# Two attention layers on one core: float32r softmax sums, a two-part order for the last batch, a separate block for the first normalisation, and weight sums by VectorE

## The chip, the core and the metric

The kernel runs on one core of one Trainium2 chip. A time is the device time of one execution, in microseconds (us). Engines are named as in the profile: PE is TensorE's matmul queue and PEld its weight loads, DVE is VectorE, ACT is ScalarE, POOL is GpSimd, SP is SyncE, which here only issues transfers.

## What is computed

The input is x of shape 8 x 32 x 32 x 512, float32: 8 batches of N = 1024 tokens with C = 512 channels. Two layers follow each other; each adds to x an attention over a normalised x. The normalisation has 32 groups of 16 channels and no learned scale.

```python
x = x + L0(group_norm(x))     # qkv = xn @ w_qkv; 16 heads of 32; softmax(q k^T / sqrt(32)) v; @ w_proj + b_proj
x = x + L1(group_norm(x))     # q, k, v = xn @ Wq, Wk, Wv; 4 heads of 128;
                              # softmax(q k^T / sqrt(128) + relative position logits) v; @ Wo
```

## The kernel before, in words

**Products.** All eight 512 x 512 products of a batch (q, k, v and the projection of each layer) are done as 2 x 2 block products with seven multiplications instead of eight. The activations need four combined blocks, made by four VectorE operations in `forms` (L327, operations L339 to L342); the weights need four sums each, made once by `Matrix.add_up` (L137, operation L146) and stored to DRAM, from where `Stream` (L167) fetches the tiles that each product needs, seven products ahead, on SyncE's queue (L193, L197). The first layer's three matrices are kept on chip for the first batch (`keep`). `seven` (L348) runs the seven products of one half in the order of `ORDER`, 0, 5, 1, 4, 6, 2, 3, into three PSUM banks x, y and z; VectorE, ScalarE and GpSimd drain them (`Plain` L405 and `Onto` L430). Products 0 and 1 read only the blocks a11 and a12, which are the activations themselves; 5, 4, 6, 2 and 3 read at least one combined block or a block of the second half of the tokens.

**Attention.** `attention_0` (L526) works on four heads at once: 8 score matmuls (L539) into a four-bank PSUM tile `ps`, one exponential on ScalarE (L547), 4 matmuls with v (L558), and a VectorE addition that keeps the sum of the exponentials (L567, L569). `attention_1` (L644) works on one head and 512 queries: for each of 8 blocks of 128 keys, a score matmul (L654, float32), a matmul that adds the position logits (L655, float32r: the constant `sel` and `posT`), an exponential (L657), a matmul with v (L666) and an addition (L675, L677). When the 8 blocks are done, `finish` multiplies the exponentials' sums by a matrix of ones (L686, float32), which adds them over partitions, and `normalise` (L496) turns them into reciprocals and multiplies (L502 to L524).

**Order.** Round b of the loop at L958 runs the first layer's attention of batch b beside everything else (`side_by_side`, L883): the projection of batch b-1 (`after_0`), the output projection of batch b-2 (`after_1`), the second layer's q, k, v of batch b-1 (`second`), its attention, and the loading and q, k, v of batch b+1. `side_by_side` takes steps from the rest according to costs that each part yields (2 for each pair of matmul groups); the second attention yields 0, so outside the round b = 7 it runs without first-layer steps in between. In round 7 its first 32 of 64 blocks run beside the first attention; in round 8 there is no first attention at all. `woven` (L871) mixes a side part into a main part at a given start and gap. Within these limits each engine's queue is put in order by when work is expected to be ready, and `issue_after` adds that an instruction comes after a given one on its engine.

**Start and end.** `load_first` (L726) brings batch 0 as rows, transposes them on PE, copies them with ScalarE and VectorE (L752, L754), takes statistics (L249), stores x (`put_away`, L214), normalises in place (L294) and makes the forms. Then the sums of WV0 are made by GpSimd, those of WQ0 and WK0 by VectorE (L939 to L942). `before_first` runs the first halves of v, q and k. The sums of the other five matrices are made by GpSimd during the q, k, v of batch 1 (`other_sums`, L946, woven at L1002). At the end `after_1` projects the last batch: forms, then twice seven products, each output block being transposed by VectorE (L856) and stored by four DMAs (L861).

Large tensors sit in eight blocks of 2 MB (`block`), so a new one waits for a free block.

Of the kernel before, what the change touches and what calls it, by code (L numbers as in the profile page):

```python
# [17 lines left out]
P = 128  # L18
# [9 lines left out]
def quick_path(  # L28
# [58 lines left out]
    ones = consts.tile([P, P], F32, tag="ones", name="ones")  # L87
    nc.gpsimd.memset(ones, 1.0)
# [28 lines left out]

    HC, HN = CC // 2, NB // 2
# [5 lines left out]
    class Matrix:  # L124
# [12 lines left out]
        def add_up(self, engine, store, keep=False):  # L137
# [5 lines left out]
            for i, (x, y) in enumerate(  # L143
                [(b12, b11), (b22, sums[:, 0]), (b22, b12), (b21, sums[:, 1])]
            ):
                engine.tensor_tensor(sums[:, i], x, y, op=ALU.subtract)  # L146
# [18 lines left out]
    ORDER = [0, 5, 1, 4, 6, 2, 3]  # L165

# [46 lines left out]

    def put_away(xT, name):  # L214
        kept = []
        for cc in range(CC):
            d = dram.tile([P, N], F32, tag="kept", name=f"d_{name}_{cc}", bufs=4 * CC)
            nc.sync.dma_start(d, xT[cc])
            kept.append(d)
        return kept  # L220
# [34 lines left out]
    def group_norm(st, xT, name, after=None, behind=None):  # L255
# [36 lines left out]
        for cc in range(CC):  # L292
            with tc.issue_after(behind().ins) if behind is not None else nullcontext():
                nc.vector.tensor_scalar(  # L294
                    xT[cc],
# [13 lines left out]
    half_done = [None]  # L309

# [16 lines left out]
    def forms(x, name, room=None):  # L327
# [11 lines left out]
        nc.vector.tensor_add(s1, a21, a22)  # L339
        nc.vector.tensor_sub(s2, s1, a11)  # L340
        nc.vector.tensor_sub(a21, a11, a21)
        nc.vector.tensor_sub(s4, a12, s2)  # L342
        return [a11, a12, s4, a22, s1, s2, a21]

# [3 lines left out]
    def seven(fs, u, rows, sink, name, hook=None):  # L348

# [17 lines left out]

        x = bank(f"x_{name}")
# [31 lines left out]
        yield HC  # L403

# [239 lines left out]
    def attention_1(q, k, v, posT, b):  # L644
# [15 lines left out]
        def back(h, c, j, e):  # L660
# [15 lines left out]
            elif j > 1:  # L676
                nc.vector.tensor_add(state["esum"], state["esum"], e)  # L677
# [5 lines left out]
        def finish(h, c, esum):  # L683
            name = f"1_{b}_{h}_{c}"
            su = bank(f"sums_{name}")
            nc.tensor.matmul(su, ones, esum, start=True, stop=True)  # L686
            normalise(q[:, h, c * NB : (c + 1) * NB], su, name)

        pending = None
        for at in steps:  # L690
            e = front(*at)
            ended = state.pop("ended", None)
# [3 lines left out]
            if ended is not None:  # L696
                finish(*ended)
# [3 lines left out]
        finish(*state.pop("ended"))  # L701

    def load(b, st):
# [3 lines left out]
        ahead = [load_blocks(b, *parts[i]) for i in range(2)]  # L707
# [15 lines left out]
        st["xn"] = forms(x, f"xn0_{b}")  # L723
        yield 0

    def load_first(st):  # L726
# [5 lines left out]
        WV0.fetch(nc.sync)  # L732
        x = block("x0T_0")
        xT = chunks(x)
        for h in range(NH):
# [13 lines left out]
            for cc in range(CC):  # L749
                part = xT[cc][:, h * NB : (h + 1) * NB]  # L750
                if h == 0 or cc % 2:
                    nc.scalar.copy(part, banks[cc])  # L752
                else:
                    nc.vector.tensor_copy(part, banks[cc])  # L754
# [4 lines left out]
        for cc in (1, 0, 3, 2):  # L759
            statistics(st, xT, cc, "0_0")  # L760
        st["kept"] = put_away(xT, "0_0")
        run(group_norm(st, xT, "0_0"))
        st["xn"] = forms(x, "xn0_0")
# [42 lines left out]
    def after_0(b, st, hook=None):  # L806

        fs = st.pop("ao0") if "ao0" in st else forms(st["q0"], f"ao0_{b}", block(f"forms_{b}"))
        x = st["x1"] = block(f"x1T_{b}")
        xT = fetch(st["kept"], x)  # L810
        for u in range(2):
            bias = [bproj_sb[:, n * HC + u : n * HC + u + 1] for n in range(2)]
            stream.unit(WP, False, u)
            yield from seven(
                fs, u, False, Onto(halves(xT, u), bias), f"wp_{b}_{u}", hook if u else None
            )
            for n in range(2):
                statistics(st, xT, n * HC + u, f"1_{b}")

# [25 lines left out]
    def after_1(b, st, hook=None):  # L845

        if "ao1" not in st:
            forms_1(b, st)
        fs = st.pop("ao1")
        xT = fetch(st["kept"], block(f"x2T_{b}"))  # L850
        for u in range(2):

            def put_out(n, h):
                m = n * HC + u
                ot = mem.tile([P, NB], F32, tag="row", name=f"ot_{b}_{m}_{h}", bufs=3)
                nc.vector.transpose(ot, xT[m][:, h * NB : (h + 1) * NB])  # L856
                ot = ot.rearrange("p (t i) -> p t i", i=32)
                for a in range(P // 32):

                    queue = nc.scalar if b == B - 1 and a % 2 else nc.sync  # L860
                    queue.dma_start(  # L861
                        by_blocks(of[b, h * NB : (h + 1) * NB, :], m * P + 32 * a),
                        ot[32 * a : 32 * a + 32],
                    )

            stream.unit(WO, False, u)
            yield from seven(
                fs, u, False, Onto(halves(xT, u), then=put_out), f"wo_{b}_{u}", hook if u else None
            )

# [50 lines left out]

    FIRST = units(WQ0) + units(WK0) + units(WV0, True)
    plan = [(m, m is WV0, u, ORDER) for u in range(2) for m in (WV0, WQ0, WK0)]
    for b in range(B + 1):
        if b >= 1:
            plan += units(WP)
# [8 lines left out]
    plan += units(WO)  # L935
# [3 lines left out]
    WV0.add_up(nc.gpsimd, nc.gpsimd, keep=True)  # L939
    for m in (WQ0, WK0):  # L940
        m.fetch(nc.sync)
        m.add_up(nc.vector, nc.gpsimd, keep=True)  # L942
# [3 lines left out]
    def other_sums():  # L946
        for m in (WP, WQ1, WK1, WV1, WO):
            m.fetch(nc.gpsimd)
            m.add_up(nc.gpsimd, nc.gpsimd)
# [7 lines left out]
    run(before_first(states[0]))  # L957
    for b in range(B + 1):  # L958
# [11 lines left out]
        if last is not None:  # L970
# [14 lines left out]
            attention = later(lambda st: attention_1(*st.pop("at")), last)  # L985
            if here is not None and coming is None:
# [8 lines left out]
            rest.append(woven(attention, incoming, 4, 6))  # L995
# [3 lines left out]
        if coming is not None:  # L999

            before = later(before_0, b + 1, coming, forms_0 if last is not None else None)
            rest.append(before if last is not None else woven(before, other_sums(), 2, 7))  # L1002
# [500 lines left out]
```

## Time and profile before

| | |
|---|---|
| runs of the kernel | 3879.32, 3877.97, 3873.93 us; median 3877.97 |
| the profiled execution, its own time | 3877.0 us |
| its span | 3875.2 us |
| mean granted PE clock | 0.996 |
| first q, k, v product (x_v, L315) starts | 27.28 us |
| first step of the first attention (ps, L539) | 67.39 us |
| last product of the last projection begins | 3863.08 us |

Busy shares are in the page's first part. A busy PE is not a PE at its peak: matmuls are pipelined and their ends are modelled, so how fast they go is read from the distance of their starts. The waits of PE list the time in which PE had nothing in flight, with what ended it. The chain of waits goes back from the last instruction to what released it.

### The profile page before, as it was taken

To read this page: it belongs to the slowest core of one execution; us is meant where nothing else is said; L and a number is where in the kernel's file an instruction comes from. 1 tells how busy PE (TensorE), PEld (TensorE's weight loads), DVE (VectorE), ACT (ScalarE), POOL (GpSimd) and SP (SyncE) were. 2 spreads that over 40 slices of the span, in tenths; PEclk is the share of its full clock that TensorE was granted. 3 is DMA by queue.
4 is the path that set the end of the run, shared out by engine and by line. 5 is a ranking of instruction groups with operands and counts; after the bars stand their busy time and mean duration, and the time that the engine had idled before them with its cause. 6 is when DMAs were issued, how large, how long until landed. Compare 5 with 4: busy or idle time off the path is not lost.

```text
span 3875.2 us, 79813 instructions
## 1 busy us (share of the span) xinstructions
PE 3803.0 (98%) x34478; PEld 1375.0 (35%) x34478; DVE 2516.4 (65%) x2905; ACT 1723.9 (44%) x1767; POOL 625.1 (16%) x400
## 2 busy tenths in 40 slices
PE   8999999999999999999999999999999999999998
PEld 3222244232443234432343323433234332334353
DVE  6777765686745867468664686656866568665544
ACT  2554543545434454344544445444453445553232
POOL 2242101121001211012111121111210112001101
PEclk9999999999999999999999999999999999999999
DMA  6122120142202322033120241103311023110401
GB/s 183 58 87 80 42 60 3 37 126 65 57 6 79 94 54 55 12 92 87 42 55 17 92 94 38 47 21 98 90 41 39 27 97 76 34 52 24 121 17 23
DMA packets 482984, 234.73 MB, mean 61 GB/s; under 512 B 269600, under 2 KB 461376, under 8 KB 481600
## 3 DMA queue, kind: packets, MB, share of 16 engines
q1 hardware_dynamic: 470992, 213.74, 20.4%
q0 software_dynamic: 2608, 13.70, 1.0%
q8 instruction: 274, 4.49, 0.5%
q10 hardware_dynamic: 9024, 2.10, 0.3%
q14 instruction: 86, 0.70, 0.1%
HBM read 170.72 MB, written 58.72 MB: 59 GB/s over the span
## 4 chain that ended last, share of the span: by engine, by line
PE 87%; DVE 8%; ACT 2%; issue 2%; DMA 0%; SPq 0%; POOL 0%; DVEq 0%; ACTq 0%; POOLq 0%
PE ps L539 12%; PE ps L654 11%; PE acc L666 11%; PE acc L558 11%; PE y_q L315 4%; PE y_v L315 4%; PE y_k L315 4%; PE ps L655 3%; PE x_q L315 3%; PE z_k L315 3%; PE x_v L315 3%; PE x_k L315 3%; PE z_q L315 3%; PE z_v L315 3%; DVE es L569 2%; ACT e L547 2%
## 5 line engine op out<-in xcount | busy, mean ns | idle before, releaser
L547 ACT ACTIVATE e<-ps 128x2048 f32<-128x2048 f32 x512 | 961.6, 1878 | 839.3 <-PE ps L539 628.2
L569 DVE TENSOR_TENSOR es<-es,e 128x2048 f32<-128x2048 f32 x384 | 893.3, 2326 | 408.6 <-ACT e L547 405.6
L539 PE MATMUL ps<-q,k 32*64 32x512 f32 x8192 | 576.6, 614 | 18.4 <-ACT e L547 18.4
L657 ACT ACTIVATE e<-ps 128x512 f32<-128x512 f32 x512 | 305.7, 597 | 573.8 <-PE ps L655 537.8
L558 PE MATMUL acc<-e,v 128*32 128x512 f32 x4096 | 545.9, 605 | 0.0
L654 PE MATMUL ps<-q,k 128*128 128x512 f32 x1024 | 525.2, 595 | 0.3 <-DVE posT L640 0.3
L666 PE MATMUL acc<-e,v 128*128 128x512 f32 x1024 | 522.0, 593 | 0.0
L524 POOL TENSOR_TENSOR q<-q,su 128x512 f32<-128x512 f32 x128 | 216.3, 1690 | 1556.8 <-DVE su L520 1538.0
L677 DVE TENSOR_TENSOR es<-es,e 128x512 f32<-128x512 f32 x384 | 290.6, 757 | 252.8 <-ACT e L657 250.8
L655 PE MATMUL ps<-posT,sel 128*128 128x512 f32 x512 | 407.0, 795 | 0.0
L654 PEld LDWEIGHTS ps<-q,k 128*128 128x128 f32 x1024 | 192.9, 190 | 250.4 <-issue 243.8
L539 PEld LDWEIGHTS ps<-q,k 32*64 32x64 f32 x8192 | 120.3, 130 | 409.8 <-issue 221.1
L666 PEld LDWEIGHTS acc<-e,v 128*128 128x128 f32 x1024 | 193.5, 190 | 146.3 <-issue 105.0
L558 PEld LDWEIGHTS acc<-e,v 128*32 128x32 f32 x4096 | 81.5, 108 | 412.0 <-issue 364.7
L567 DVE TENSOR_TENSOR es<-e,e 128x2048 f32<-128x2048 f32 x64 | 172.9, 2701 | 33.2 <-ACT e L547 33.2
L504 DVE STREAM_TRANSPOSE tu<-su 128x512 f32<-128x512 f32 x128 | 90.6, 708 | 121.7 <-ACT su L502 120.1
L502 ACT COPY su<-sums 128x512 f32<-128x512 f32 x128 | 74.9, 585 | 149.0 <-PE sums L579 81.2
L655 PEld LDWEIGHTS ps<-posT,sel 128*128 128x128 f32 x512 | 97.5, 190 | 122.3 <-issue 122.3
L640 DVE TENSOR_TENSOR posT<-pp,posT 32x512 fp32r<-32x512 f32 x128 | 112.0, 875 | 32.3 <-ACT posT L635 31.0
L675 DVE TENSOR_TENSOR es<-e,e 128x512 f32<-128x512 f32 x64 | 44.2, 691 | 135.8 <-ACT e L657 135.8
L428 POOL TENSOR_TENSOR k<-b_k,p_k 128x512 f32<-128x512 f32 x32 | 51.9, 1623 | 483.6 <-ACT p_k L393 483.6
L635 ACT CAST posT<-pp 32x512 fp32r<-32x512 f32 x128 | 106.2, 829 | 46.3 <-PE pp L622 45.1
(200 smaller groups left out, 4449.4 us busy)
## 6 DMA issues: line engine op xcount, KB each, us to landing
w_qkv<-ws_qkv SPq DMA_DIRECT2D x168, 128.0 KB, 2.5
d<-x0T SPq DMA_DIRECT2D x32, 512.0 KB, 3.6
x1T<-d SPq DMA_DIRECT2D x32, 512.0 KB, 5.4
d<-x1T SPq DMA_DIRECT2D x32, 512.0 KB, 3.4
x2T<-d SPq DMA_DIRECT2D x32, 512.0 KB, 6.0
w_qkv<-in_L_conv_w_qkv SPq DMA_DIRECT2D x126, 128.0 KB, 2.2
out<-ot SPq DMA_DIRECT2D x240, 64.0 KB, 2.0
xs<-in_x SPq DMA_DIRECT2D x224, 64.0 KB, 2.5
```

What stands on the lines that cost most here:

```text
L315: ins = nc.tensor.matmul(out[columns, :], weights[:, columns], moving, start=start, stop=stop, skip_group_check=open_sum,)
L524: nc.gpsimd.tensor_tensor(dst, dst, su, op=ALU.mult)
L539: nc.tensor.matmul(ps[some, r, :], k[m][rows, j * P + 64 * i : j * P + 64 * i + 64], q[m][rows, h * NB : (h + 1) * NB], start=True, stop=True,
L547: nc.scalar.activation(e, ps, AF.Exp, scale=D0 ** -0.5)
L558: nc.tensor.matmul(acc[r * D0 : (r + 1) * D0, :], v[:, j, c0 : c0 + D0], e[:, r, :], start=(j == blocks[0]), stop=(j == blocks[-1]),)
L567: nc.vector.tensor_add(state["esum"], state["first"], e)
L569: nc.vector.tensor_add(state["esum"], state["esum"], e)
L654: nc.tensor.matmul(ps, k[h][:, keys], q[:, h, queries], start=True, stop=False)
L655: nc.tensor.matmul(ps, sel_flat[:, keys], posT[:, h, queries], start=False, stop=True)
L657: nc.scalar.activation(e, ps, AF.Exp, scale=1.0 / math.sqrt(D1))
L666: nc.tensor.matmul(acc, v[:, j, h * D1 : (h + 1) * D1], e, start=(j == 0), stop=(j == NT - 1),)
L677: nc.vector.tensor_add(state["esum"], state["esum"], e)
```

## The change

1. **Float32r sums.** `ones` is a float32r tile. In `attention_1`, where no first attention runs beside, `finish` becomes a generator: one block after the end ScalarE casts the sums to float32r (`greater`), VectorE subtracts that from the sums (`rest`), two blocks later two float32r matmuls add both over partitions into one PSUM tile, now in the slot of `ps`. The form before stays for the sums that end while `beside` holds.
2. **Two-part order.** For the last batch's output projection (`after_last`) and the first batch's first projection, products 0 and 1 of both halves come before the forms, the other five of both halves after them.
3. **Late output.** The output blocks of batch 6 (B - 2) are transposed and stored during the last attention instead of directly after each product.
4. **First batch.** The three first matrices are fetched directly after the rows, all copies are made by ScalarE, the statistics go in the order of the copies, the normalised x goes to a block of its own, the loads of batch 1 are put behind the stores of batch 0.
5. **Weight sums.** WV0's last two sums move from GpSimd to VectorE; VectorE's sums are put behind the last operation of the forms before them. The sums of WK0 and of the other five matrices are made by VectorE in between the products of `before_first`, from fetches and with stores on SyncE's queue.
6. **Forms in steps.** When a batch is loaded, the four operations of its forms are separate steps, each behind the latest addition of the second attention; the weave of loading into attention has a gap of 5 instead of 6.

```diff
-    ones = consts.tile([P, P], F32, tag="ones", name="ones")
-    nc.gpsimd.memset(ones, 1.0)
+    ones_r = consts.tile([P, P], F32R, tag="ones", name="ones")
+    nc.gpsimd.memset(ones_r.bitcast(F32), 1.0)
+    ones = ones_r.bitcast(F32)
...
+                engine = engines[i]
+                with tc.issue_after(last_form[0].ins) if engine is nc.vector else nullcontext():
+                    engine.tensor_tensor(sums[:, i], x, y, op=ALU.subtract)
...
+    FIRST_TWO, LAST_FIVE = [0, 1], [5, 4, 6, 2, 3]
...
+    def in_two_parts(x, m, sinks, name, room=None, done=lambda u: None):
+        early = [x[:, :HC, :NB], x[:, HC:, :NB]]
+        p1s = []
+        for u in range(2):
+            stream.unit(m, False, u)
+            p1s.append((yield from two_first(early, u, sinks[u], f"{name}_{u}")))
+        fs = forms(x, name, room)
+        for u in range(2):
+            stream.unit(m, False, u)
+            yield from five_last(fs, u, sinks[u], f"{name}_{u}", p1s[u])
+            done(u)
...
-            su = bank(f"sums_{name}")
-            nc.tensor.matmul(su, ones, esum, start=True, stop=True)
+            if (h * NH + c + 1) * NT < beside:
+                su = bank(f"sums_{name}")
+                nc.tensor.matmul(su, ones, esum, start=True, stop=True)
+                normalise(q[:, h, c * NB : (c + 1) * NB], su, name)
+                return
+            yield
+            greater = mem.tile([P, NB], F32R, tag="rec", name=f"sg_{name}", bufs=2)
+            nc.scalar.copy(greater, esum)
+            rest = mem.tile([P, NB], F32R, tag="rec", name=f"sr_{name}", bufs=2)
+            nc.vector.tensor_sub(rest, esum, greater.bitcast(F32))
+            yield
+            yield
+            su = psum.tile([P, HB, NB], F32, tag="ps", name=f"sums_{name}", bufs=1)[:, 0, :]
+            nc.tensor.matmul(su, ones_r, greater, start=True, stop=False)
+            nc.tensor.matmul(su, ones_r, rest, start=False, stop=True)
             normalise(q[:, h, c * NB : (c + 1) * NB], su, name)
...
-        WV0.fetch(nc.sync)
+        for m in (WV0, WQ0, WK0):
+            m.fetch(nc.sync)
...
-            for cc in range(CC):
+            for cc in (0, 2, 1, 3):
                 part = xT[cc][:, h * NB : (h + 1) * NB]
-                if h == 0 or cc % 2:
-                    nc.scalar.copy(part, banks[cc])
-                else:
-                    nc.vector.tensor_copy(part, banks[cc])
+                nc.scalar.copy(part, banks[cc])
...
-        run(group_norm(st, xT, "0_0"))
-        st["xn"] = forms(x, "xn0_0")
+        xn = block("xn0_0")
+        run(group_norm(st, xT, "0_0", out=chunks(xn)))
+        st["xn"] = forms(xn, "xn0_0")
...
+        def put_later(n, h):
+            st.setdefault("late", []).append(lambda: put(n, h))
+        return put_later if b == B - 2 else put
...
-    WV0.add_up(nc.gpsimd, nc.gpsimd, keep=True)
-    for m in (WQ0, WK0):
-        m.fetch(nc.sync)
-        m.add_up(nc.vector, nc.gpsimd, keep=True)
+    WV0.add_up([nc.gpsimd] * 2 + [nc.vector] * 2, nc.gpsimd, keep=True)
+    WQ0.add_up([nc.vector] * 4, nc.gpsimd, keep=True)
...
     def other_sums():
+        WK0.add_up([nc.vector] * 4, nc.gpsimd, keep=True)
+        yield 0
         for m in (WP, WQ1, WK1, WV1, WO):
-            m.fetch(nc.gpsimd)
-            m.add_up(nc.gpsimd, nc.gpsimd)
+            m.fetch(nc.sync)
+            m.add_up([nc.vector] * 4, nc.sync)
             yield 0
...
-    run(before_first(states[0]))
+    run(woven(before_first(states[0]), other_sums(), 3, 3))
...
-            rest.append(woven(attention, incoming, 4, 6))
+            if here is None:
+                incoming = later(late_output, past)
+            rest.append(woven(attention, incoming, 4, 5))
...
-            rest.append(before if last is not None else woven(before, other_sums(), 2, 7))
+            rest.append(before)
...
-    run(after_1(B - 1, states[B - 1]))
+    after_last(B - 1, states[B - 1])
```

## The prediction

> **What bounds the kernel now.** I read the engine row of the page first, then the waits of TensorE, then the chain of waits stage by stage, then the timelines around each TensorE gap.
>
> ```profile
> span 3875.2 us, 79813 instructions
> PE 3803.0 (98%) x34478; PEld 1375.0 (35%) x34478; DVE 2516.4 (65%) x2905; ACT 1723.9 (44%) x1767; POOL 625.1 (16%) x400
> PE ps L539 <- ACT e L547: 18.4, 16, 2.9
> PE x_v L315 <- issue: 10.6, 1, 10.6
> PE y_wo L315 <- DVE a_wo L379: 10.5, 7, 1.7
> PE turned L744 <- DMA x_rows<-in_x: 6.1, 3, 4.9
> PE y_wo L315 <- DVE f_ao L340: 3.1, 1, 3.1
> PE x_q L315 <- DMA w_q<-in_L_conv_Wq: 2.9, 1, 2.9
> PE y_wp L315 <- DVE forms L340: 2.5, 1, 2.5
> ```
>
> The reader is to see that TensorE stands still for only 72 us of 3875, so two things can shorten the run: fewer TensorE cycles, or closing one of these few gaps. The largest single gap (10.6 us) is at the start; 3.1 is at the end; 2.9 and 2.5 are once each.
>
> How much a matmul costs must be read from starts, because the durations overlap. In the second layer's attention, which runs alone on TensorE, the timeline (start, length) and then the chain (start, length) say:
>
> ```profile
> 3752.47 1.02 PE L686 MATMUL sums<-es,ones 128*128 128x512 f32 x2
> 3753.33 1.02 PE L654 MATMUL ps<-q,k 128*128 128x512 f32 x2
> ...
> 3801.93 0.86 PE sums L686 x2
> 3802.79 0.86 PE ps L654 x2
> 3803.65 0.23 PE ps L655
> 3803.88 0.86 PE acc L666 x2
> ```
>
> A float32 product of 512 columns is two instructions and 0.86 us; the float32r product L655 of the same shape is one and 0.23. TensorE issues these without a gap: a key block is 2 x 0.86 + 0.23 = 1.95 us and the sum L686 adds 0.86.
>
> The start, on VectorE and TensorE, and the other gaps:
>
> ```profile
> 17.39 1.65 DVE L146 TENSOR_TENSOR prep_qkv<-prep_qkv 128x512 f32<-128x512 f32 x1 [2.22 <-DMA prep_qkv<-in_L_conv_w_qkv]
> 26.36 2.98 DVE L294 TENSOR_SCALAR x0T<-x0T,back,rstd 128x1024 f32<-128x1024 f32 x4 [1.17 <-POOL rstd L290]
> ...
> 3622.43 4.13 SPq L861 DMA_DIRECT2D out<-ot  x8
> 3626.66 0.45 SPq L197 DMA_DIRECT2D w_q<-in_L_conv_Wq  x1
> 3629.09 3.62 PE L315 MATMUL x_q<-x1T,w_q 128*32 128x512 f32 x16 [2.92 <-DMA w_q<-in_L_conv_Wq]
> ```
>
> A weight sum put into VectorE's queue ahead of the statistics waits there for its transfer. Late in the run a weight tile stands in SyncE's queue behind stores of the output. The x16 product after that gap takes 3.62 us where its followers start 1.72 apart: a gap costs more than its length.
>
> **What the Trainium skill says.** "FP8 and Floating Point Precision", TensorE Precision Notes: true FP32 takes four passes through the array. The trace agrees: 0.86 against 0.23, a ratio of 3.7. "TensorE: Matmul & The Clock Gate", What's actually happening: after an idle window of about 3.4 us the array runs at half clock for about as long. The trace agrees roughly: the windows table gives a granted clock of 0.66 in 330-340 us, where the 2.5 us gap lies, and the product after it took 3.64 instead of 1.72. "SBUF — State Buffer", Who interferes with whom: a VectorE instruction with two SBUF inputs contends with a GpSimd instruction that reads SBUF. The trace agrees: at 163.38, while GpSimd forms weight sums (10.51 us for four), two L569 additions took 9.38 us where one takes 2.29. "Perfetto Trace Analysis", the note on the Tensor Engine's lifecycle: VectorE, ScalarE and GpSimd are strict FIFO. The wait at 17.39 with the statistics behind it agrees.
>
> **The change part by part**, against the profiled execution's own 3877.0 us (span 3875.2; the median of the runs is 3877.97, so 1.0 is added at the end).
>
> *Float32r sums.* The second attention has 8 sums in each of 8 batches; the three that finish while the first attention still runs beside keep the old form (batch 6), so 61 change. Each loses one 0.86 and gains two 0.23: 0.40 saved, 61 x 0.40 = **24.4 us**, all of it on TensorE's path since the stage has no gap (the waits of TensorE between 560 and 800 us are empty). Added: one cast on ScalarE (0.59, from L680) and one subtraction on VectorE (0.69, from L677) per 8 blocks. ScalarE idles about 1.35 us and VectorE 1.25 per block, and the sum is now issued two blocks (3.9 us) later than before, so both are hidden; queued behind the cast are exponentials, whose consumer has 1.8 us of slack (e ends at 3752.41, L666 reads it at 3754.42). Without cover it would be 1.3 us each. At the end of a batch's attention there is no later block: the two matmuls wait 1.3 us there; other products stand ready, so I take 0, with 8 x 1.3 = 10 as the far bound. If the loads of the ones (190 ns) did not overlap, the pair would cost 0.84 and save nothing; L655's load of the same length is hidden, so I take 0.46. The sum moves to the slot of the first attention's scores; no first-attention step is issued inside this stage, so I cost that at 0, and at one copy (0.58) per batch if it is.
>
> *Start.* VectorE's weight sums are put behind the forms, the copies go to ScalarE, three weight fetches follow the rows directly and the next batch's 128-byte-wide loads (xs, issued from 4.98) come later. Statistics ended at 22.28; out of their way go the wait and blocked time 15.17-19.08 (3.9), the sums between (3 x 0.6 = 1.8) and the two copies (1.29): 7.0. One more 0.57 sum inside the small operations goes, and between the normalisation and the first y product VectorE has two sums less (29.26 and 31.00, 1.2). The added ScalarE copies (2 x 0.54) cost up to 1.1 on the other side, and the reordering of statistics may win 1.5. Sum: **9 us**, bounds 5 to 12. The separate block by itself is worth 0 in this trace (the normalisation at 26.36 waited for rstd, not for the store); it stops the store from being late next.
>
> *Other weights' sums between the first products.* 24 VectorE sums of 0.65 = 15.6 us move into about 36 us of products (WK0's four were already there late), where VectorE is busy 12 to 13 of 25 us. Two of WV0's go to VectorE too. Behind each group of four (2.6 us) stands a drain of y; TensorE has one other product (1.72) before it needs that, so 0.9 us is lost for a bad meeting: 6 x 0.9 = 5.4; 0 if they fall well. Each also waits for a 1 MB fetch (5.5 to 13.2 us to land); that wait is the slower rival below. SyncE issues 5 fetches and 5 stores more, with w tiles queued behind that are first read near 144 us. I take **4 us lost**, bounds 0 to 20. In return GpSimd's 20 sums between 149 and 276 us go: the 1.82 and 0.67 us gaps beside them end, **2.5 gained** (0 to 6).
>
> *First batch's projection in two parts.* Before y_wp there are gaps of 1.04 and 2.50, and the next two groups run slow (3.64 for 1.72, 1.80 for 1.04): 6.2 in all. Two more products (3.44 us) now lie ahead of the forms. I take **4** (0 to 6); c11 now waits for the fetched x1T ahead of the forms if it is queued first, which is the 0.
>
> *Stage 3560-3700.* Batch 6's 8 transposes (0.7) and 32 stores go into the last attention, which has VectorE idle 1.25 per block and SyncE idle. The w_q gap (2.92 plus 1.90 of slow clock) goes, and the second a_wo gap (1.74, two transposes just ahead of it): **6.5** (3 to 7). The first a_wo gap, 1.63, stays.
>
> *End.* The gap before y_wo is 3.1, plus 1.6 of slow product; two products (3.44) move into it, but the last sum comes 1.1 us later by the cast and the subtraction. PE ended at 3865.0 with 12 products after the forms; now 10 follow. **3.5** (0 to 5). The 10 us of draining after it stay.
>
> *Forms step by step and a gap of 5 in the weave:* 12 pieces now fit where 9 did; TensorE had no wait there: 0.
>
> Sum: 24.4 + 9 - 4 + 2.5 + 4 + 6.5 + 3.5 = 45.9; 3877.0 - 45.9 + 1.0 = **3832 us**.
>
> **Rivals.** (1) *Slower: the sums' fetches hold VectorE.* While the first products run, seven of the eight blocks are live (xn, three kept weights, v, q, k), so the five matrices pass through one block in turn: fetch 8.8 + sums 2.6 + store 7.3 = 18.7 us a round (medians of the wqkv rows). If VectorE stands in its queue at each, four rounds take 75 us where twelve products take 20.6: 54 lost, plus 4 x 1.9 of slow clock = 62, against 49.9 of gains: **3890**. It decides above a round of 15.7 us; with 5.8 + 2.6 + 4.3 = 12.7 (the quiet transfers' landing) it would lose 38 and leave 3866. Against it: VectorE's queue is arranged by when work should be ready, the fetches can start early, and the wait at 17.39 was 2.2, not 18. (2) *Start given back:* shorter stalls of this sort, and later work pushed into 75-100 us, where VectorE is busy 23.9 of 25, cost about 20 instead of 4: **3848**. For it: the added VectorE work is real and in order. (3) *The float32r pair saves nothing* because its loads or the cast come on the path: 3832 + 24 = **3856**. Against it: L655. (4) *Everything falls well*, no stall in the sums and the upper ends of start and projection: **3820**.
>
> **Chances.** Forecast 0.52; (2) 0.20; (3) 0.06; (4) 0.12; (1) 0.10, of which 0.07 end slower and 0.03 within 0.2% or a little faster. Range 3816 to 3858: it holds the forecast and (2) to (4), leaving (1) and tails. 0.2% (7.8 us) is about what a measurement of this kernel can tell from no change. Faster 0.90, same 0.03, slower 0.07.
>
> **What would show it.** Right: the sums in the second attention as two single-instruction matmuls 0.23 apart and eight blocks in 16.0 us instead of 16.4; normalisation (L294's counterpart) at 17 to 19 us; first x_v at 18 to 20; no w_q wait near 3600; no GpSimd weight sums after 140; four x products ahead of the last forms. Wrong: VectorE waiting for prep transfers between 25 and 90 us with TensorE gaps behind; first attention step later than about 60 us (it is at 67.4 now); gaps ahead of the second layer's sums.

## The result, and the profile after

| | before | after |
|---|---|---|
| median of the runs | 3875.47 us (8 runs, 3873.12 to 3879.32) | 3862.96 us (8 runs, 3861.07 to 3866.5) |
| ratio, 95% interval | 1 | 0.9968 [0.9957, 0.9978] |
| span of the profiled execution | 3875.2 us | 3859.2 us |
| first x_v product | 27.28 us | 19.42 us |
| first step of the first attention (ps) | 67.3 us | 61.6 us |

The kernel became 12.5 us faster. The forecast was 46 us and the range began at 3816 and ended at 3858: the sign was right, the size a quarter, and the time lies 5 us above the range. From the page of the kernel after, its span and engine row, and then TensorE's waits (us in total, times, longest):

```profile
span 3859.2 us, 79885 instructions
PE 3788.9 (98%) x34478; PEld 1374.0 (36%) x34478; DVE 2562.2 (66%) x2986; ACT 1760.1 (46%) x1830; POOL 573.4 (15%) x368
PE ps L623 <- ACT e L631: 26.7, 18, 6.6
PE y_wo L327 <- DVE a_wo L411: 8.7, 6, 1.6
PE x_v L327 <- issue: 3.5, 1, 3.5
PE y_v L327 <- DVE b_v L419: 2.8, 1, 2.8
PE y_wp L327 <- DVE a_wp L455: 2.6, 2, 1.8
```

The gap ahead of x_v fell from 10.6 to 3.5, and the waits for w_q and for the last forms are gone. Two waits for drains on VectorE are new, those of y_v and y_wp, and the wait of the first attention's scores for the exponentials grew from 18.4 to 26.7, with one of 6.6 us where the longest was 2.9. The float32r pair runs as forecast. The chain of waits in batch 0's second attention (start, length), first in the middle and then at its end:

```profile
660.67 0.86 PE acc L750 x2
661.53 0.23 PE sums L786
661.76 0.24 PE sums L787
662.00 0.86 PE ps L738 x2
...
668.93 1.81 PE acc L750 x4
670.74 0.98 PE x_q L327 x2
671.72 0.44 PE sums L786
672.15 0.23 PE sums L787
```

In the middle, 0.47 stands where 0.86 stood. At the end the next product x_q has begun, stops after two of its matmuls, and the pair comes before the rest.

Where the 16.0 us of span went (the two traced executions are further apart than the medians) is read from landmarks: the start of the same matmul in both traces. Each row is how much the kernel after was ahead of the one before (+) when the stretch ended, and what the stretch added.

| stretch | ahead at its end | the stretch gave | predicted |
|---|---|---|---|
| to the first x_v | 7.9 | +7.9 | +9 |
| to step 16 of the first attention (142 us) | -9.0 | -16.8 | -4 |
| to round 1 (331 us): GpSimd's weight sums gone | -6.4 | +2.6 | +2.5 |
| to batch 0's second attention (542 us): projection in two parts | -5.2 | +1.2 | +4 |
| to round 7 (3152 us): six batches of float32r sums | 6.1 | +11.2 | +19.2 |
| to the end of batch 6's attention (3554 us) | 5.2 | -0.9 | +2.0 |
| to batch 7's attention (3690 us): late output | 10.9 | +5.7 | +6.5 |
| to its end (3816 us): eight float32r sums | 13.6 | +2.7 | +3.2 |
| to the end of the run | 16.0 | +2.4 | +3.5 |

Most of what is missing lies in two places: the stretch up to 142 us (12.8) and the three stretches of the float32r sums (11.4 together).

The start did what was forecast. The normalisation on VectorE and the first product on TensorE, in the timeline of the kernel after (start, length; the idle time before and its releaser in brackets):

```profile
18.50 2.98 DVE L304 TENSOR_SCALAR xn<-x0T,back,rstd 128x1024 f32<-128x1024 f32 x4 [1.16 <-POOL rstd L300]
19.42 3.56 PE L327 MATMUL x_v<-prep_qkv,xn 128*32 128x256 f32 x32 [3.50 <-issue]
```

26.36 became 18.50 and 27.28 became 19.42. The loss comes later. The chain of waits of the kernel after between 65 and 85 us, where the last two of the five matrices pass through one block:

```profile
65.05 4.67 DMA ws_v<-prep_v
69.75 0.03 issue
69.78 5.98 DMA prep_o<-in_L_conv_Wo
...
75.84 1.89 DVE prep_o L152 x3
...
78.96 5.32 DMA ws_o<-prep_o
```

Each line begins where the one before lets it: store, then fetch into the same block, then the sums, then store. Not all five matrices pass through this block, as the prediction had it. The chain has the fetch of prep_q, and SyncE's timeline the issue of the next fetch while it is under way:

```profile
36.83 10.88 DMA prep_q<-in_L_conv_Wq
...
40.17 0.39 SPq L138 DMA_DIRECT2D prep_k<-in_L_conv_Wk  x1
```

So two blocks take part. prep_q, prep_v and prep_o follow each other in one, in rounds of 17.9, 15.0 and 14.6 us, and batch 1's x comes next in it; prep_p and prep_k have the other, and batch 0's k comes next in that (e10 below shows both hand-overs as waits). This is what VectorE does behind the last fetch, by its timeline:

```profile
75.84 1.89 DVE L152 TENSOR_TENSOR prep_o<-prep_o 128x512 f32<-128x512 f32 x3 [4.17 <-DMA prep_o<-in_L_conv_Wo]
77.65 0.68 DVE L419 TENSOR_TENSOR b_v<-y_v,p_v 128x512 f32<-128x512 f32 x1
78.25 0.68 DVE L152 TENSOR_TENSOR prep_o<-prep_o 128x512 f32<-128x512 f32 x1
78.85 3.37 DVE L653 TENSOR_TENSOR es<-es,e 128x2048 f32<-128x2048 f32 x1
84.40 1.30 DVE L823 STREAM_TRANSPOSE x0T<-xs 128x512 f32<-128x512 f32 x2 [2.18 <-DMA ws_o<-prep_o]
...
112.23 3.94 DVE L304 TENSOR_SCALAR x0T<-x0T,back,rstd 128x1024 f32<-128x1024 f32 x4 [1.22 <-POOL rstd L300]
116.09 0.70 DVE L588 STREAM_TRANSPOSE tu<-su 128x512 f32<-128x512 f32 x1
...
117.85 2.25 DVE L651 TENSOR_TENSOR es<-e,e 128x2048 f32<-128x2048 f32 x1
```

TensorE's two gaps there, and VectorE's first transposes of batch 1 in the kernel before:

```profile
78.39 1.93 PE L327 MATMUL y_v<-prep_qkv,f_xn 128*32 128x256 f32 x32 [2.81 <-DVE b_v L419]
...
122.12 2.02 PE L623 MATMUL ps<-q,k 32*64 32x512 f32 x16 [6.64 <-ACT e L631]
```

```profile
59.57 1.29 DVE L717 STREAM_TRANSPOSE x0T<-xs 128x512 f32<-128x512 f32 x2
```

The drain b_v stands behind the fetch of prep_o and three of its sums, and y_v waits for it. Batch 1's x gets the block only when the last weight's store has landed: its first transpose begins at 84.40, where it was 59.57 in the kernel before, although the attention now begins 5.7 us earlier. VectorE stands there for 2.18 us, and from then to 111 us the timeline lists no idle time ahead of any of its instructions. The first attention's reciprocal sums (L588) and its next addition (L651, at 117.85) come behind batch 1's normalisation, and TensorE's gap of 6.6 us ends at 122.12, once that addition has let an exponential go.

### The profile page after: what moved, and what is told of

The parts are those of the page before. It is cut to its first block, busy times and chain, and to the rows that moved or that the text cites. A ratio compares the mean times of both kernels' runs of the same rounds, so it can differ in the third digit from the quotient of the medians.

```text
span 3859.2 us, 79885 instructions
## 1 busy us (share of the span) xinstructions
PE 3788.9 (98%) x34478; PEld 1374.0 (36%) x34478; DVE 2562.2 (66%) x2986; ACT 1760.1 (46%) x1830; POOL 573.4 (15%) x368
## 4 chain that ended last, share of the span: by engine, by line
PE 85%; DVE 9%; ACT 2%; issue 2%; DMA 1%; POOL 0%; SPq 0%; DVEq 0%; ACTq 0%; POOLq 0%
PE ps L623 12%; PE ps L738 11%; PE acc L750 11%; PE acc L642 11%; PE y_k L327 4%; PE y_q L327 4%; PE y_v L327 4%; PE ps L739 3%; PE z_k L327 3%; PE x_q L327 3%; PE x_v L327 3%; PE x_k L327 3%; PE z_q L327 3%; PE z_v L327 2%; DVE es L653 2%
## 5 line engine op out<-in xcount | busy, mean ns | idle before, releaser
L623 PE MATMUL ps<-q,k 32*64 32x512 f32 x8192 | 578.7, 613 | 26.7 <-ACT e L631 26.7
L651 DVE TENSOR_TENSOR es<-e,e 128x2048 f32<-128x2048 f32 x64 | 171.5, 2680 | 32.5 <-ACT e L631 32.4
L588 DVE STREAM_TRANSPOSE tu<-su 128x512 f32<-128x512 f32 x128 | 90.5, 707 | 94.6 <-ACT su L586 93.0
L512 POOL TENSOR_TENSOR v<-b_v,p_v 128x512 f32<-128x512 f32 x32 | 52.9, 1654 | 459.4 <-ACT p_v L425 433.5
```

Of the source, the lines that this page charges most:

```text
L623: nc.tensor.matmul(ps[some, r, :], k[m][rows, j * P + 64 * i : j * P + 64 * i + 64], q[m][rows, h * NB : (h + 1) * NB], start=True, stop=True,
L651: nc.vector.tensor_add(state["esum"], state["first"], e)
```

## The experiments

Each time is a median, with the ratio to the kernel before on the same chip and its 95% interval (the medians of the kernel before were 3875.2 to 3875.9, close enough to set medians of different experiments against each other to within about 1 us). Diffs are against the changed kernel where nothing else is said.

### Undoing the weight sums' move: e1_sums_gpsimd

```diff
+    WK0.add_up([nc.vector] * 4, nc.gpsimd, keep=True)
...
-        WK0.add_up([nc.vector] * 4, nc.gpsimd, keep=True)
-        yield 0
...
-            m.fetch(nc.sync)
-            m.add_up([nc.vector] * 4, nc.sync)
+            m.fetch(nc.gpsimd)
+            m.add_up([nc.gpsimd] * 4, nc.gpsimd)
...
-    run(woven(before_first(states[0]), other_sums(), 3, 3))
+    run(before_first(states[0]))
...
-            rest.append(before)
+            rest.append(before if last is not None else woven(before, other_sums(), 2, 7))
```

> The changed kernel with one part undone: the sums of the five other matrices are made by GpSimd during the products of batch 1, as before, and those of WK0 directly after those of WQ0; all else is kept. Theory (the sums between the first products pass through one block in turn, hold VectorE's queue and delay the loading of batch 1): the first attention's step 16 of batch 0 comes about 6 us before that of the kernel before instead of 9 us after it, some 14 us better there; the 2.6 us that the absence of GpSimd's sums had given are lost again, so the run is about 3851 us (12 less than the changed kernel). Rival (the loss after 62 us comes from putting the loads of batch 1 behind the stores of batch 0, or from the normalisation's own block): step 16 stays 7 to 9 us late and the run is within 3 us of 3863, or above.

Measured: **3847.0**, 0.9927 [0.991, 0.9943]: 16 us below the changed kernel. At step 16 of the first attention this kernel's trace is 15.9 us ahead of it; by round 1 it has lost 2.1 of that again and by batch 0's second attention 2.4. So the move as a whole costs 15.9 and gives 2.4 back, where the prediction had 4 and 2.5.

### VectorE in the old place: e2_sums_vector_later

As e1, but `m.fetch(nc.sync)` and `m.add_up([nc.vector] * 4, nc.sync)` kept, in the old place.

> As the run with the sums undone, but VectorE makes the sums of the five matrices, from fetches and with stores on SyncE's queue, during the products of batch 1 where GpSimd made them before. Theory (the place is what costs, not the engine): step 16 of batch 0 as early as with GpSimd's sums, and [...] the round ends 1 to 3 us earlier than with them: about 3849 us. Rival (15 us of VectorE work cost about as much wherever they are put): step 24 and later are 5 us or more behind the run with GpSimd's sums, 3857 us or more.

Measured: **3867.6**, 0.998 [0.9972, 0.9988]. My theory failed: VectorE costs 20.6 us in the old place too. Between 100 and 345 us VectorE's waits name three fetches, and TensorE has two gaps ahead of products that wait for drains, which e1 has not:

```profile
DVE prep_o L152 <- DMA prep_o<-in_L_conv_Wo: 5.3, 1, 5.3
DVE prep_k L152 <- DMA prep_k<-in_L_conv_Wk: 5.0, 1, 5.0
DVE prep_p L152 <- DMA prep_p<-in_L_conv_w_proj: 3.9, 1, 3.9
```

```profile
PE ps L623 <- ACT e L631: 11.6, 7, 4.5
PE y_k L327 <- DVE b_k L419: 5.4, 1, 5.4
PE y_q L327 <- DVE b_q L419: 4.2, 1, 4.2
```

The scores' wait for the exponentials is 10.6 in e1, but its longest is 2.9 there and 4.5 here.

### The float32r sums alone: e3_f32r_alone

The kernel before with the new `finish` of `attention_1` and the float32r `ones`, nothing else.

> The kernel before with only the float32r sums and the new way of finishing. The prediction's term: 61 x 0.40 = 24.4 us less, 3851 against 3875.5. Theory (inside a stage each sum saves 0.39; at the end of each batch's attention the pair waits and about 1.2 us are lost; in the round with the first attention beside, the old-form sums now come one block earlier and lose 0.8 each): -2.0 us for each of batches 0 to 5, about +1 for batch 6, -2.5 for batch 7, together about 13 to 14 us: 3862. Rival (the sums' place in the slot of the first attention's scores costs too): less than 10 us.

Measured: **3872.9**, 0.9994 [0.9985, 1.0002]: no gain that can be told from zero, where 24 was forecast. The waits of TensorE have a line that the kernel before has not and the changed one only once, with 0.3 us, and the timeline shows one of its six places (columns as above):

```profile
PE acc L668 <- ACT e L659: 7.3, 6, 1.3
```

```profile
1060.09 2.30 DVE L343 TENSOR_TENSOR x0T<-x0T 128x1024 f32<-128x1024 f32 x1
...
1064.82 0.62 ACT L696 CAST sg<-es 128x512 fp32r<-128x512 f32 x1 [3.31 <-DVE es L679]
1065.34 0.59 ACT L659 ACTIVATE e<-ps 128x512 f32<-128x512 f32 x1
...
1065.99 1.13 PE L668 MATMUL acc<-e,v 128*128 128x512 f32 x2 [1.21 <-ACT e L659]
```

Two forms of the next batch's load (2.30 and 1.21 us) hold up the additions on VectorE. Before, nobody waited for an addition within a block. Now the cast on ScalarE does, for 3.31 us, an exponential is queued behind the cast, and TensorE waits for that.

### The last sum in the old form: e4_last_sum_f32

```diff
-            if (h * NH + c + 1) * NT < beside:
+            if (h * NH + c + 1) * NT < beside or h * NH + c == H1 * NH - 1:
```

> The changed kernel, with the last sum of each batch's second attention in the old float32 form (in a bank, directly after the last block), the other 53 in float32r. Theory (the last pair waits for the cast, the subtraction and the copy queued beside them, with nothing else to issue): about 1.2 us less in each of batches 0 to 6, 0.5 to 1.2 in batch 7, so 8 to 9 us less than the changed kernel, 3854. Rival (the pair would be hidden, and the 1.2 us at the end come from the first attention's next step having to wait for the slot): the same by this edit if the slot is the cause, but then the next first-attention step waits for its scores' slot in the trace of the changed kernel; second rival (the loss is only a shift of work): within 2 us of the changed kernel.

Measured: **3855.2**, 0.9947 [0.993, 0.9964], 7.7 below the changed kernel. A batch now gains about 2.7 on the kernel before, and not about 2.0. The end of batch 0's attention in this kernel's chain of waits:

```profile
671.20 1.81 PE acc L750 x4
673.01 0.86 PE sums L771 x2
673.87 1.85 PE x_q L327 x16
```

From the last acc to the first scores behind it (676.59) it is 5.39 us; in the changed kernel it was 6.16 (668.93 to 675.09). So the pair costs 0.77 more than the old sum at the end of an attention. It waits there for ScalarE, whose copy L764 and cast come after the last acc (the trace puts 6.7 us of idle time ahead of the pair, in 8 places, down to that copy), and x_q stands behind it.

### VectorE's work without the transfers: e9_work_alone

e1, and VectorE makes 20 subtractions of the same size between the first products, from WQ0's kept block into a scratch tile.

> The changed kernel with the five other matrices' sums back on GpSimd in their old place (3847 measured for that alone), and VectorE doing 20 subtractions of the same size between the first products, from weights that are already on chip and into a scratch tile: its 13 us of work without any transfer to wait for. This is added work whose result nothing uses. My theory, that the 16 us lost there come from VectorE standing in its queue on fetches and stores that pass through one block in turn: at most 3 us more than 3847, so 3847 to 3850. The rival, that VectorE's 15.6 us of added work by itself costs it because it stands in order ahead of the products' drains and of batch 1's loading: 3857 to 3863.

Measured: **3847.4**, 0.9925 [0.9908, 0.9941]: 0.4 more than without them. VectorE in its timeline, from the middle of them to batch 1's first transposes:

```profile
36.00 4.17 DVE L1101 TENSOR_TENSOR scratch<-prep_qkv 128x512 f32<-128x512 f32 x5
...
52.71 1.29 DVE L823 STREAM_TRANSPOSE x0T<-xs 128x512 f32<-128x512 f32 x2
```

The added work is all but hidden: of the "bad meetings" of sums with drains, from which the prediction's 4 us came, this trace has one, in which y_q waits 0.7 us for its drain a_q. Batch 1 begins at 52.71 here. The test has a limit. With no fetch to wait for, the 20 subtractions are done by 50.3 us, while the changed kernel's sums come as late as 79. Two of the meetings do occur there, behind the sums of prep_q and prep_k:

```profile
50.28 1.92 PE L327 MATMUL y_k<-f_xn,prep_qkv 128*32 128x512 f32 x16 [0.64 <-DVE q L505]
...
54.61 1.92 PE L327 MATMUL y_k<-f_xn,prep_qkv 128*32 128x512 f32 x16 [0.69 <-DVE a_k L411]
```

### The three edits together: e5_best

After with the edits of e1 and e4 and, for the old-form sums of round 7, a `yield` ahead of them.

> The changed kernel with three edits: the five other matrices' sums by GpSimd in their old place, the last of each attention's eight sums in the old float32 form, and the old-form sums of round 7 one block later. Sum of what the runs give: 3847.0 - 8 x 0.78 - 2.4 = 3838. If the edits get in each other's way (the gaps that the last sum's form removed come back elsewhere): 3844 or more. Clearly below both kernels in either case.

Measured: **3838.5** (3837.39 to 3839.28), 0.9902 [0.9886, 0.9919]. The gains add up, and this is the fastest version: 37 us below the kernel before, 24.5 below the changed one.

### The float32r sums with their guard: e6_f32r_and_steps

e3 with two more parts of the change: the forms of a loaded batch as steps, each behind the latest addition, and the gap of 5.

> The kernel before with the float32r sums, with the forms of a loaded batch in single steps behind the additions, and with a gap of 5 in the weave; nothing else of the change. My theory, that the float32r sums alone gained only 2 us because the cast on ScalarE waited for an addition which four forms in a row had held up, with the exponentials queued behind it: the steps remove that 1.5 us of each batch, so about 13 us below the kernel before, 3862. The rival, that the gain of the float32r sums is lost in another place: within 3 us of the float32r sums alone, 3870 to 3875.

Measured: **3865.8**, 0.9974 [0.9965, 0.9984], 10 below the kernel before and 7.1 below e3, where 13 and 11 were expected. The wait of acc for the exponentials fell from 7.3 us to 0.3, and a batch gains about 2.0 in the trace, as in the changed kernel.

### The late output alone: e8_late_output_alone

The kernel before with batch 6's transposes and stores kept back and woven into the last attention.

> The kernel before with only batch 6's output transposes and stores put into the last attention. By the traces of before and after the wait for w_q and the slow product after it go, and one wait for a_wo: 5.7 us of the 6.5 that I predicted, so 3869 to 3870. If that gain in the changed kernel belonged to another part of the change (its waits shifted by it): within 2 us of the kernel before.

Measured: **3869.5**, 0.9984 [0.9977, 0.9991], 6.3 below the kernel before. The trace has 5.4 of it in the stretch from 3559 to 3701 us, and the wait for w_q is gone.

### GpSimd in VectorE's place: e10_gpsimd_in_place

```diff
-            m.add_up([nc.vector] * 4, nc.sync)
+            m.add_up([nc.gpsimd] * 4, nc.sync)
```

> The changed kernel with one word different: the 20 sums of the five other matrices by GpSimd instead of VectorE, still between the first products and with fetches and stores on SyncE's queue. My theory, that the loss is VectorE standing on transfers: GpSimd can stand there instead, since what is queued behind it (one drain from on-chip tiles for each product, the reciprocal root of batch 1) is needed late, so nearly the whole loss goes: 3847 to 3852. The rival, that the transfers themselves in this place are the cost (one block in turn, weight tiles and batch 1's loading queued behind on SyncE): it stays at 3859 to 3863.

Measured: **3877.9**, 1.0006 [0.9997, 1.0015]: 15 above the changed kernel. Both theories missed, mine by more. What I had overlooked is in VectorE's waits of this kernel between 30 and 160 us:

```profile
DVE x0T L823 <- DMA ws_o<-prep_o: 14.6, 1, 14.6
DVE k L505 <- DMA ws_k<-prep_k: 9.2, 1, 9.2
```

With another engine making the sums, VectorE stands all the same, 23.8 us, for the blocks that the weights have in turn: k of batch 0 and x of batch 1 are next in them. GpSimd takes 5.1 us for a group of four where VectorE takes 2.6, so the last store ends at 93.9 instead of 84.3.

### The old-form sums one block later: e7_beside_late

After with `yield` as the first statement of the old-form branch of `finish`.

> The changed kernel with one step more ahead of the old-form sums, which in round 7 are issued one block earlier than in the kernel before. My theory, that each of these sums now waits for its addition, 0.8 to 1.2 us apiece: 2 to 3 us below the changed kernel's 3863, so 3860 to 3861. If the later place pushes another wait into the first attention's steps there: no gain or a loss of up to 2.

Measured: **3861.1**, 0.9963 [0.9949, 0.9977]. The median is 1.9 lower, and the intervals overlap. In the trace round 7 shows it: from step 48 to the end of batch 6's attention the changed kernel loses 0.8 on the kernel before, this one gains 1.6, so 2.4 is the sum's place. The old-form sum had come one block early, because the generator's first step runs it at once.

### Batch 1's loading late, without a transfer to wait for: e12_loaded_late and e13_loaded_later

The kernel of e1 with batch 1's transposes put behind the third (e12) or fifth (e13) addition of the first attention on VectorE (`ADDS` lists those additions):

```diff
-            nc.vector.transpose(xT[cc][:, h * NB : (h + 1) * NB], xs)
+            with tc.issue_after(ADDS[2].ins) if b == 1 else nullcontext():
+                nc.vector.transpose(xT[cc][:, h * NB : (h + 1) * NB], xs)
```

> The changed kernel with the five other matrices' sums by GpSimd in their old place (3847 alone), and batch 1's transposes put behind the third of the first attention's additions on VectorE, so that they begin near 83 us, where they began at 84.40 in the changed kernel, and not before 55. Nothing waits for a weight's transfer here. My new theory, after GpSimd in VectorE's place lost even more: the five matrices pass through one block in turn, batch 1's x gets that block only after the last store, and its loading, which then crowds VectorE, is what costs. So most of the 16 us come back: 3857 to 3864. The rival, that the standing of VectorE itself or the transfers cost: 3846 to 3850.

> As the run before, with the transposes behind the fifth addition, near 92 to 94 us, where they began with GpSimd making the sums between the first products (94.18). By the theory of late loading: some 9 us more than with the third addition, as 9.8 us of later handing on went with 9 us of later attention there: 3866 to 3873. By the rival: 3846 to 3850 again.

Measured: **3850.1**, 0.9935 [0.9918, 0.9951], and **3850.3**, 0.9936 [0.9919, 0.9952]: 3.1 and 3.3 above e1. So late loading costs something, but not 16, nor more in the later of these two places; the second theory fell too.

### Two matrices instead of five: e11_two_matrices

After with WP and WQ1 between the first products by VectorE, WK1, WV1 and WO by GpSimd in the old place.

> The changed kernel with only the first two of the five matrices (the first layer's projection and the second layer's q) between the first products by VectorE, the other three by GpSimd in the old place. The block is handed on after two rounds instead of five, some 25 us earlier. By the theory of late loading nearly all of the loss goes, though VectorE still stands on the second fetch (4.2 us in the changed kernel): 3847 to 3851. By the theory that VectorE's standing costs, two of the three stands remaining in part: 3852 to 3858.

Measured: **3851.3**, 0.9938 [0.9921, 0.9954]: 4.3 above e1 and 11.7 below the changed kernel. The landmarks against e1 show 1.7 lost by the attention's first step, 0.8 more by step 8, and the rest later in rounds 0 and 1.

### The queue or the engine, in the old place: e14_sync_queue

e1 with `nc.sync` for the fetches and stores; GpSimd makes the sums.

> The changed kernel with the five other matrices' sums by GpSimd in the old place, their fetches and stores on SyncE's queue instead of GpSimd's; it differs from the run of VectorE in the old place (3867.6) by the engine alone, and from GpSimd in the old place (3847.0) by the queue alone. If that run's 20.6 us came from VectorE standing on the fetches (three of 3.9 to 5.3 us): 3847 to 3850. If they came from the transfers on SyncE's queue, with weight tiles behind them: 3860 to 3868.

Measured: **3846.8**, 0.9927 [0.9911, 0.9944], as e1. The transfers on SyncE's queue cost nothing there; the 20.6 us of e2 belong to VectorE alone, which stood 14.2 us on three fetches with the first attention's additions behind it. The landmarks of the two traces tell the standing from the work: e2 falls behind e14 by 7.0, 8.1 and 5.6 us in the steps of the three stands (22 to 24, 36 to 38, 50 to 52), and by nothing from step 44 to 50, where VectorE makes the four sums of prep_v, whose fetch had landed. The sums that follow directly on a stand can't be told from it.

### The additions first, transfers kept: e15_additions_first

The changed kernel itself with the edit of e12: the weight sums stay between the first products.

> The changed kernel itself, weight sums by VectorE between the first products as they are, with one edit: batch 1's transposes stand behind the third of the first attention's additions on VectorE, which also puts the reciprocal sums of the first attention ahead of batch 1's last statistics. My third theory, after late loading alone cost only 3 us, VectorE's work alone none, and two matrices 4: the cost is an order of VectorE's queue that is right only if the block comes early; when five rounds through it put that off to 84 us, VectorE stands at the first transpose and then does 24 us of loading ahead of additions and sums that TensorE waits for. With the additions first about 9 of the 16 us come back, the loss at the drain behind the last fetch (3.0), the start (1.2) and 3 of late loading stay: 3852 to 3856. The rival, that the transfers and stands on them cost wherever loading stands: 3860 to 3863.

Measured: **3855.3**, 0.9947 [0.993, 0.9964]: 7.7 of the 16 come back, by an order alone. In the traces, steps 5 to 16 take 45.5 us here, just as in e12, where the changed kernel takes 54.5 and e1 42.9: in this stretch 9.0 come back. Before it, this trace is 2.2 us later than the changed kernel's. What is left of TensorE's waits between 30 and 150 us (line numbers are one higher here; in the changed kernel the second of these waits came to 8.6 us between 60 and 145, the first to 2.8):

```profile
PE y_v L328 <- DVE b_v L420: 2.9, 2, 2.7
PE ps L624 <- ACT e L632: 2.2, 2, 1.5
```

## Why the size was wrong, point by point

- **Start:** right. 9 forecast, 7.9 measured at x_v. 1.2 us of it are lost again by the attention's first step, against e1.
- **Other weights' sums: the step that failed.** The prediction took 4 us for six meetings of a group of sums with a drain; what the sums' fetches and stores do to VectorE's queue it put at nothing in that sum, and its first rival asked only whether VectorE would stand at each fetch. Measured is 15.9. Against e1 in the landmarks: 1.2 before the attention begins, where two of the meetings show (0.64 and 0.69); 3.0 at y_v, whose drain stands behind the fetch of prep_o (4.2 us of VectorE's standing); and 11.7 between steps 5 and 12. Of those 11.7, late loading by itself is 2.7 (e12's landmarks, up to step 16). The other 9 are the order of VectorE's queue behind a block that comes late, with the 2.2 us of standing at the first transpose: e15 changes that order alone and gets 9.0 back in this stretch, 7.7 in the median.

  The prediction had seen that nearly all blocks are live; it counted one block for five matrices where the trace has two, and did not ask who takes them next. One goes to batch 1's x, and VectorE's order, made for a block that comes near 52 us, puts its loading ahead of additions that TensorE waits for. The added work, which the 4 came from, costs 0.4 where no transfer holds it (e9). The prediction's own sign of being wrong, VectorE waiting for prep transfers with TensorE gaps behind, came true twice (4.20 and 4.17 us). Rival (2), "start given back" with 3848, named the right place and a like size for the loss; on its own terms it would have been wrong mainly by the float32r term.
- **GpSimd's sums gone:** the size came out, 2.5 forecast and 2.6 measured, but the cause isn't shown. In e14 GpSimd makes the same sums in the old place, and its trace takes 188.9 us from step 16 to round 1, like the changed kernel's (188.8); e1's takes 190.9 and that of the kernel before 191.5.
- **Float32r sums:** the saving was mis-sized at both ends. Within a batch each of seven sums saves 0.39, as forecast (0.40). The eighth costs 0.77 more than the old form, where I took 0 "since other products stand ready": the product that stands ready is begun and then held behind the pair. My far bound of 10 for eight batches was the right one to take: 8 x (0.40 + 0.77) = 9.4. In round 7, where I took only five of batch 6's eight sums as changed, the three unchanged ones came one block earlier and cost 2.4 (e7's trace); I had not read what the generator's first step does. 24.4 - 9.4 - 2.4 = 12.6; measured in the three stretches 13.0.
- **Forms in steps and the gap of 5:** I costed them at 0 because TensorE had no wait there before. They are the cover of the float32r sums: without them the cast waits (e3), with them it doesn't (e6), and that is 7.1 us (for both parts together; e6 does not tell them apart). I had costed the loss of cover at "1.3 us each" and not asked which VectorE work could take it away.
- **Two-part projection:** 1.2 of 4. The products wait now for a_wp (2.6 in two times) instead of for the forms.
- **Late output:** right, 5.7 of 6.5, and 6.3 alone (e8).
- **End:** 2.4 of 3.5; a wait of 1.0 for a_wo stands where the 3.1 was.

The terms that failed were each inside their own bounds (0 to 20, and 0 to 10), and both fell to the far side. I treated them as if only one could go wrong. Put right together they give 3832 + 11.9 + 9.4 + 2.4 = 3856; the two-part term's 2.8 and the 3.0 of start, late output and end make 3862, against 3863 measured. That they meet so closely is partly luck: the sum explains the two traced executions, which are 16 us apart where the medians are 12.5 apart, and it starts from the median of three runs, 2.5 above that of eight.

**What stays open:** how much of e2's 20.6 us is the work that follows directly on its three stands, why e13's later loading costs no more than e12's, and what gave the 2.6 us after step 16.

## What to carry to other kernels

Where a step is moved to an earlier place and uses a buffer, ask who takes that buffer next, when the step will hand it on, and what stands on the in-order queue behind that taker; here the work itself cost 0.4 us where nothing held it, and the move as a whole four times the estimate. When an off-path operation becomes one that another engine waits for (here an addition, for a cast), whatever could delay it harmlessly before has to be moved out of its way in the same change. A saving per repetition is to be checked at the last repetition, where the work that covers it has ended.

## What the runs showed of the hardware

- Fetches of the same 1 MB took 10.88 us (prep_q, from 36.83) and 5.98 (prep_o, from 69.78) in one execution. Around the first, SyncE had issued loads of xs and the fetch of prep_k; that these made the difference is a reading, and no run tries it.
- A gap does not always slow TensorE's next product. After one of 2.81 us (y_v at 78.39) the product took 1.93 us, as long as the one before it (1.91), where in the kernel before the product after 2.92 us took 3.62. After the 6.6 us gap the scores took 2.02 instead of 1.04 and the products with v 1.51 instead of 1.00. "TensorE: Matmul & The Clock Gate", What's actually happening, in the Trainium skill puts the idle window at about 3.4 us: the 6.6 and the 2.81 agree with it, the 2.92 doesn't. Nor does the 2.50 ahead of y_wp, with 3.64 behind it, which the prediction took as rough agreement.
